# Two layers of graph attention in f32: q, k and v of two batches in one product, weight pieces fetched from DRAM as they are used

## The chip, the cores and the metric

One core of a Trainium2 chip. The time is device microseconds of one execution, the median of three: 2844.64 us for the kernel before (2844.39 to 2846.03). All numbers are f32; nothing is computed in a narrower type.

## What is computed

64 batches of 256 tokens with 512 features pass two layers:

```python
q, k, v = x @ Wq + bq, x @ Wk + bk, x @ Wv + bv          # 8 heads of 64
scores = q k^T / 8 + (1 - adj) * -1e9                     # 256 x 256 a head
x = layernorm(x + softmax(scores) v @ Wo + bo)
h = x @ W;  s1 = h a1;  s2 = h a2
e = leaky_relu(s1[:, None] + s2[None, :], 0.2) * adj
x = layernorm(x + elu(softmax(e) h + beta h))
```

Five products with a 512x512 matrix are taken per batch: q, k, v, o and u. The second layer mixes x by its softmax first, with beta on the diagonal ("spread"), and multiplies by W after ("u"); W a1 and W a2 are folded into two rows once.

## The kernel before

**Seven products for eight.** A 512x512 product is split in halves on three sides (features in, features out, tokens); by a Strassen-Winograd scheme it takes seven products of halves in place of eight. The left sides (weights) are W11, W12, W22 and four sums; weight_sums (line 337) makes the sums once and keeps them in SBUF, and writes W21 + W22 over W21. The right sides are quarters of the transposed tokens xT and three sums of them, made per batch by token_sums (line 351) with four subtractions on GpSimd. project (line 370) runs the seven products into three PSUM tiles (chain, cross, pair), each followed by a copy (ACT) or an add (DVE) into a quarter of the result. For q and k the result lies by feature: the stationary side is a 128x128 block of the weights and 128 tokens stream past it, four matmuls a product (line 383). For v, o and u the tokens are stationary and 256 features stream, two matmuls a product (line 388). Only batch 0's q and k are taken the plain way (plain_qk, line 550).

**A batch's stages.** x (transposes of x, L535), q, k, scores (eight heads, two at a time in two row halves of the array, L637), exp and mask on ACT and DVE, v, sums (denominators by a matmul with ones, L660; reciprocal on DVE; out to DRAM and back on every partition by three DMAs of SP, L675 and L679), mix (weights times v, L614), o, normalization (L482 to L492), logits (L813 on DVE, L823 on PE), softmax, attention (L859), spread, u, finish (L516 to L522).

**The order.** Nothing is issued as it is written. Every step is recorded with Plan.op: its engine, a cost in ns, the buffers it reads, writes and claims. Plan.place (line 107) then puts them in order. PE's order is given: each PE step belongs to a turn (round, place in ROUND), and line 503 says in which round after its own a stage of batch b runs (x two rounds early, q and k one early, u two late), so that one round holds stages of five batches and every result has other stages to hide behind. All other engines are filled by a list scheduler: earliest start first, then the due time that follows from PE's order. Buffers come from pools with a fixed number of slots (line 236: 9 of the size of a 256x512 tile, 24 of half that, 8 PSUM banks); a step waits for a slot. The last 60 PE steps are free of the turns. SP issues all large DMAs in one queue, in the order that place gives.

One round takes 43.77 us, the same to 0.01 us from batch to batch. From the timeline of PE, with the start of each stage: sums 1400.67, mix 1401.67, scores 1405.28, q 1408.93, attention 1415.29, v 1415.72, spread 1421.77, o 1424.92, u 1430.96, k 1437.01, x 1443.26, logits 1444.13, next sums 1444.44.

**Beginning and end.** The first round loads x and the weights, makes the weight sums, res_sb (bo + bv Wo, residual_bias, line 438, four matmuls of 128x512), the mask and the second layer's rows. The last batch takes plain products for o and u and spreads its reciprocals by matmul. If any denominator is out of range, a second pass in another form follows; it does not run here.

The lines that set the old order:

```python
ROUND = ("sums", "mix", "scores", "q", "attention", "v", "spread", "o", "u", "k", "x", "logits")
...
            later = {"x": -2, "q": -1, "k": -1, "scores": 0, "v": 0, "sums": 1, "mix": 1, "o": 1, "logits": 1,
                     "attention": 2, "spread": 2, "u": 2}[what]
            plan.turn = (n + later, ROUND.index(what))
```

Of the kernel before, what the change touches and what calls it, by code (L numbers as in the profile page):

```python
# [11 lines left out]
AF = mybir.ActivationFunctionType  # L12
# [4 lines left out]
P = 128  # L17
# [5 lines left out]
ROUND = ("sums", "mix", "scores", "q", "attention", "v", "spread", "o", "u", "k", "x", "logits")  # L23
# [199 lines left out]
def gnn_two_layers(ctx: ExitStack, tc: tile.TileContext, x, adj, Wq, bq, Wk, bk, Wv, bv, Wo, bo, W, a, beta, out):  # L223
# [12 lines left out]
    slots = {"x": 5, "full": 9, "half": 24, "xS": 4, "st": 90, "ps": 8, "rows": 4}  # L236
# [42 lines left out]

    def weight(w, name):  # L280
        w_sb = once([C, D], name)
        for c in range(C):
            plan.op("SP", 1000, lambda c=c: nc.sync.dma_start(w_sb[:, c], w[blk(c), :]), [], [(w_sb, c)])
        return w_sb
# [18 lines left out]
    wq_sb = weight(Wq, "wq_sb")  # L303
    wk_sb = weight(Wk, "wk_sb")
# [46 lines left out]
    def token_sums(T, keys, name):  # L351

        S = sb("xS", [3, 2, P], name)
        q = {(k, j): (lambda k=k, j=j: T[:, 2 * k:2 * k + 2, blk(j)]) for k in range(2) for j in range(2)}
        t2, t3, t4 = ((lambda i=i: S[:, i]) for i in range(3))

        def sub(dst, p, m, reads, writes):  # L360
            plan.op("POOL", 725, lambda: nc.gpsimd.tensor_tensor(dst(), p(), m(), ALU.subtract), reads, writes)  # L361

        sub(t3, q[1, 1], q[0, 1], [keys(1, 1), keys(0, 1)], [(S, 1)])
        sub(q[0, 1], q[0, 1], q[0, 0], [keys(0, 1), keys(0, 0)], [keys(0, 1)])
        sub(t2, q[1, 1], q[0, 1], [keys(1, 1), keys(0, 1)], [(S, 0)])
        sub(t4, q[1, 0], t2, [keys(1, 0), (S, 0)], [(S, 2)])
        return [(q[0, 0], [keys(0, 0)]), (q[1, 0], [keys(1, 0)]), (q[1, 1], [keys(1, 1)]), (t4, [(S, 2)]),
                (q[0, 1], [keys(0, 1)]), (t2, [(S, 0)]), (t3, [(S, 1)])]

    def project(left, right, by_feature, claims, copy, add, inner=2):  # L370

        shape = [2, P] if by_feature else [F]
        chain, cross, pair = ps(shape, "ps_chain"), ps(shape, "ps_cross"), ps([2] + shape, "ps_pair")

        def product(n, dst, start):
            l, r = left[n - 1][0](), right[n - 1][0]()
            if by_feature:  # L380
                for f in range(2):
                    for c in range(inner):
                        nc.tensor.matmul(dst[:, f, :], l[:, c, blk(f)], r[:, c, :],  # L383
                                         start=start and f == 0 and c == 0, stop=c == inner - 1,
                                         skip_group_check=True)
            else:
                for c in range(2):
                    nc.tensor.matmul(dst, r[:, c, :], l[:, c, :], start=start and c == 0, stop=c == 1,  # L388
                                     skip_group_check=True)

        def pe(n, buf, part, start, after=()):
            acc = (lambda: buf[A]) if part is None else (lambda: buf[:, part])
            key = (buf, part)
            plan.op("PE", 448 * inner if by_feature else 870, lambda: product(n, acc(), start),
                    left[n - 1][1] + right[n - 1][1] + list(after), [key], claims=claims)
            return key, acc

        copy((0, 0), pe(1, chain, None, True))
        copy((1, 1), pe(5, cross, None, True))
        add((0, 0), pe(2, pair, 0, True))  # L400
        copy((0, 1), pe(6, chain, None, False))
        add((0, 1), pe(3, cross, None, False))
        copy((1, 0), pe(4, pair, 1, False, [(pair, 0)]))
        acc = pe(7, chain, None, False)
        add((1, 1), acc)
        add((1, 0), acc)

# [30 lines left out]
    def residual_bias():  # L438
        bo_sb = for_now(bo, 0, "bo")
        acc = ps([D], "ps_b")  # L440

        def pe():
            for c in range(C):
                nc.tensor.matmul(acc[A], bv_sb[:, c:c + 1].to_broadcast([P, P]), wo_sb[:, c, :], start=c == 0,
                                 stop=c == C - 1)

        plan.op("PE", 3440, pe, [wo_sb], [acc], claims=[res_sb])
        plan.op("DVE", 690, lambda: nc.vector.tensor_add(res_sb[A], acc[A], bo_sb[A]), [acc, bo_sb], [res_sb])
        return weight_sums(wo_sb, "so_sb", "POOL", [res_sb])
# [46 lines left out]
    def batch(b, at, general=False):  # L496

        X = sb("x", [NT, D], f"x_{b}")
        n = b or 0

        def turn(what):

            later = {"x": -2, "q": -1, "k": -1, "scores": 0, "v": 0, "sums": 1, "mix": 1, "o": 1, "logits": 1,
                     "attention": 2, "spread": 2, "u": 2}[what]
            plan.turn = (n + later, ROUND.index(what))

        plan.op("SP", 2800, lambda: nc.sync.dma_start(X[A], x[at].rearrange("o (t p) d -> p (o t) d", p=P)), [],
                [(X, (t, i)) for t in range(NT) for i in range(2)], first=b == 0)

# [3 lines left out]
        def finish(t, us, u, mode):  # L513
# [9 lines left out]
                out[at].rearrange("o (t p) d -> p (o t) d", p=P)[:, t, :], X[:, t, :]), tokens(t), [])  # L523


        xT, qT, kT = (sb("full", [C, N], f"{n}_{b}") for n in ("xT", "qT", "kT"))
        last = b == B - 1 and not general
        V = sb("full", [NT, D], f"v_{b}")

        def tr_x(t):  # L530
            tr = ps([C, P], "tr_x")

            def pe():
                for c in range(C):
                    nc.tensor.transpose(tr[:, c, :], X[:, t, c * P:(c + 1) * P], ident)  # L535

            plan.op("PE", 430, pe, tokens(t), [tr], claims=[xT])
            plan.op("ACT", 680, lambda: nc.scalar.copy(xT[:, :, blk(t)], tr[A]), [tr], [(xT, t)])

            plan.op("POOL", 1270, lambda: nc.gpsimd.tensor_tensor(X[:, t, :], X[:, t, :], res_sb[A], ALU.add),  # L540
                    [res_sb], tokens(t))

        if b == 0:
            plan.turn = (0, ROUND.index("spread"))
            left["o"] = residual_bias()
        turn("x")
        for t in range(NT):
            tr_x(t)

        def plain_qk(w, bias, dst):  # L550

            accs = [ps([2, N], "ps_plain") for _ in range(2)]
            for c in range(C):
                def pe(c=c):
                    for f in range(C):
                        nc.tensor.matmul(accs[f // 2][:, f % 2, :], w[:, c, blk(f)], xT[:, c, :],  # L556
                                         start=c == 0 and f % 2 == 0, stop=c == C - 1, skip_group_check=True)

                plan.op("PE", 1740, pe, [xT, (w, c)], accs, claims=[dst])
            for f in range(C):  # L560
                plan.op("ACT", 370, lambda f=f: nc.scalar.activation(
                    dst[:, f, :], accs[f // 2][:, f % 2, :], AF.Identity, bias=bias[:, f:f + 1]),
                    [accs[f // 2]], [(dst, (f // 2, j)) for j in range(NT)])

        if b == 0:
            turn("q")
            plain_qk(wq_sb, bq_sb, qT)
            turn("k")
            plain_qk(wk_sb, bk_sb, kT)
            left["q"] = weight_sums(wq_sb, "sq_sb", "DVE")  # L570
            left["k"] = weight_sums(wk_sb, "sk_sb", "DVE")
            left["v"] = weight_sums(wv_sb, "sv_sb", "POOL")
        right = token_sums(xT, lambda k, j: (xT, j), "xS")

        def gather(quarter, bias=None):

            def copy(q, acc):
                (dst, key), (src, acc) = quarter(q), acc[::-1]
                if bias is None:
                    plan.op("ACT", 400, lambda: nc.scalar.copy(dst(), src()), [acc], [key])  # L580
                    return
                for f in range(2):
                    plan.op("ACT", 350, lambda f=f: nc.scalar.activation(
                        dst()[:, f, :], src()[:, f, :], AF.Identity,
                        bias=bias[:, 2 * q[0] + f:2 * q[0] + f + 1]), [acc], [key])

            def add(q, acc):
                (dst, key), (src, acc) = quarter(q), acc[::-1]
                plan.op("DVE", 420, lambda: nc.vector.tensor_add(dst(), src(), dst()), [acc, key], [key])  # L589

            return copy, add

        def qk(left, bias, dst):
# [404 lines left out]
```

## Time and profile before

| | |
|---|---|
| median of 3 | 2844.64 us |
| the profiled execution | 2844.93 us, its span 2843.2 us |
| granted TensorE clock | 0.998 |
| busy: PE / weight loads / DVE / ACT / POOL | 2819.6 / 2489.7 / 2092.7 / 1403.3 / 1790.3 us |
| DMA | 111.04 MB, mean 39 GB/s |
| first matmul, last start of a matmul group | 5.01 us, 2831.89 us |

PE is the matmul engine and PEld its weight loads, which run beside it. A row of the timeline is a run of like instructions: start, duration to its end, engine, line, operation, tile written <- tiles read, stationary and moving shapes, count. Each f32 matmul leaves two records, so x8 there is four matmuls of the code. Since matmuls overlap, the time of a group on PE is the distance from its start to the next start. A row of waits says which instruction waited for which: total us, how often, the longest. A row of windows gives the stretch, its length, busy time and count for PE, PEld, DVE, ACT and POOL, granted clock, share of the DMA engines, GB/s.

### The profile page before, as it was taken

The numbers are of one execution on the slowest core, as the hardware profiler recorded it, in microseconds if no ns is written. First come the engines' busy times: TensorE is split into PE (matmuls) and PEld (weight loads), VectorE is DVE, ScalarE is ACT, GpSimd is POOL, SyncE is SP. The second block draws the span as 40 slices with busy tenths as digits, with TensorE's granted clock in tenths as the row PEclk, the third lists the DMA queues.
The fourth block names the chain that finished last, engine by engine and source line by source line (L and its number), as shares of the span: only waits on it lengthen the run. The fifth ranks groups of instructions, "written<-read, shape, count | busy, mean of one in ns | idle before, by whom it ended". The sixth has DMA issues, their size and how long they took to land.

```text
span 2843.2 us, 54507 instructions
## 1 busy us (share of the span) xinstructions
PE 2819.6 (99%) x20313; PEld 2489.7 (88%) x20313; DVE 2092.7 (74%) x4498; ACT 1403.3 (49%) x3507; POOL 1790.3 (63%) x2507
## 2 busy tenths in 40 slices
PE   9999999999999999999999999999999999999997
PEld 7888888988888889888888898888888888888885
DVE  5767777777677777776777777767777777677786
ACT  4445445455454554544545545445445454454453
POOL 6666566566665665666656666666566666666654
PEclk9999999999999999999999999999999999999999
DMA  3011011011110110111101101011011010110100
GB/s 134 21 33 46 24 46 46 23 46 36 33 46 24 46 46 24 46 34 35 46 24 45 46 23 46 33 36 46 24 46 46 24 46 32 37 46 24 49 31 27
DMA packets 75645, 111.04 MB, mean 39 GB/s; under 512 B 6136, under 2 KB 39664, under 8 KB 75376
## 3 DMA queue, kind: packets, MB, share of 16 engines
q1 hardware_dynamic: 75248, 107.49, 11.7%
q8 instruction: 163, 2.67, 0.4%
q14 instruction: 106, 0.87, 0.1%
q0 software_dynamic: 128, 0.01, 0.0%
HBM read 73.41 MB, written 34.07 MB: 38 GB/s over the span
## 4 chain that ended last, share of the span: by engine, by line
PE 98%; DVE 1%; POOL 0%; issue 0%; ACT 0%; POOLq 0%; DVEq 0%
PE ps_chain L388 17%; PE ps_chain L383 15%; PE ps_cross L388 12%; PE ps_pair L388 12%; PE ps_pair L383 10%; PE ps_cross L383 10%; PE ps_sc L637 8%; PE ps_pv L614 8%; PE ps_den L660 2%; PE tr_x L535 2%; PE tr_a L859 1%; PE ps_plain L556 1%; PE tr_s L823 1%; DVE junk L813 0%; PE ps_plain L423 0%
## 5 line engine op out<-in xcount | busy, mean ns | idle before, releaser
L648 POOL TENSOR_TENSOR both<-pT 128x256 f32<-128x256 f32 x512 | 362.1, 734 | 151.6 <-ACT pT L646 151.6
L644 DVE TENSOR_TENSOR pT<-ps_sc,maskT_sb 128x512 f32<-128x512 f32 x512 | 316.8, 680 | 11.7 <-PE ps_sc L637 5.5
L580 ACT COPY u<-ps_chain 128x256 f32<-128x256 f32 x126 | 46.9, 372 | 511.3 <-PE ps_chain L388 511.3
L540 POOL TENSOR_TENSOR x<-x,res_sb 128x512 f32<-128x512 f32 x128 | 164.1, 1283 | 201.0 <-PE tr_x L535 199.8
L646 ACT ACTIVATE pT<-pT 128x512 f32<-128x512 f32 x512 | 287.2, 624 | 3.8 <-DVE pT L644 3.8
L813 DVE SCALAR_TENSOR_TENSOR junk<-x,wa_sb 128x512 f32<-128x512 f32 x256 | 261.6, 1074 | 0.0
L486 POOL TENSOR_SCALAR rs<-mv 128x1 f32<-128x1 f32 x256 | 55.4, 217 | 324.5 <-DVE mv L483 319.9
L637 PE MATMUL ps_sc<-qT,kT 64*128 64x256 f32 x2048 | 238.4, 382 | 0.0
L614 PE MATMUL ps_pv<-pT,v 128*64 128x256 f32 x2048 | 235.1, 382 | 0.0
L637 PEld LDWEIGHTS ps_sc<-qT,kT 64*128 64x128 f32 x2048 | 192.8, 187 | 44.3 <-issue 24.0
L614 PEld LDWEIGHTS ps_pv<-pT,v 128*64 128x64 f32 x2048 | 141.4, 137 | 90.7 <-issue 26.1
L492 ACT ACTIVATE x<-x,nmr,rs 128x512 f32<-128x512 f32 x256 | 194.1, 806 | 5.5 <-DVE nmr L490 5.3
L361 POOL TENSOR_TENSOR yS<-yT 128x256 f32<-128x256 f32 x126 | 91.8, 729 | 152.1 <-DVE yT L589 147.1
L482 DVE BATCH_NORM_STATS2 bn<-x 128x6 f32<-128x512 f32 x256 | 170.6, 687 | 4.4
L899 POOL TENSOR_TENSOR X_sums<-x 128x256 f32<-128x256 f32 x126 | 119.4, 948 | 85.0 <-ACT x L492 85.0
L487 POOL TENSOR_TENSOR rs<-rs,neg_half 128x1 f32<-128x1 f32 x256 | 144.3, 564 | 21.3
L700 ACT COPY oT<-ps_pv 128x512 f32<-128x512 f32 x128 | 75.0, 587 | 150.6 <-PE ps_pv L614 150.5
L790 DVE TENSOR_TENSOR x<-x,ps_chain 128x256 f32<-128x256 f32 x252 | 100.3, 418 | 63.8 <-PE ps_chain L388 56.9
L383 PE MATMUL ps_chain<-xS,sk_sb 128*128 128x128 f32 x1008 | 133.1, 275 | 0.0
L383 PE MATMUL ps_chain<-xS,sq_sb 128*128 128x128 f32 x1008 | 133.1, 275 | 0.0
L388 PE MATMUL ps_chain<-sv_sb,xS 128*128 128x256 f32 x512 | 131.4, 379 | 0.0
L388 PE MATMUL ps_chain<-sw_sb,yS 128*128 128x256 f32 x504 | 130.2, 381 | 0.0
(222 smaller groups left out, 7697.3 us busy)
## 6 DMA issues: line engine op xcount, KB each, us to landing
x<-in_x_dram SPq DMA_DIRECT2D x64, 512.0 KB, 4.5
out_dram<-x SPq DMA_DIRECT2D x128, 256.0 KB, 2.0
inv_all<-rows SPq DMA_DIRECT2D x126, 256.0 KB, 3.6
wq_sb<-in_L_gnn_Wq_dram SPq DMA_DIRECT2D x4, 256.0 KB, 5.7
wk_sb<-in_L_gnn_Wk_dram SPq DMA_DIRECT2D x4, 256.0 KB, 7.6
wv_sb<-in_L_gnn_Wv_dram SPq DMA_DIRECT2D x4, 256.0 KB, 7.4
wo_sb<-in_L_gnn_Wo_dram SPq DMA_DIRECT2D x4, 256.0 KB, 5.1
w_sb<-in_L_gnn_W_dram SPq DMA_DIRECT2D x4, 256.0 KB
```

What stands on the lines that cost most here:

```text
L383: nc.tensor.matmul(dst[:, f, :], l[:, c, blk(f)], r[:, c, :], start=start and f == 0 and c == 0, stop=c == inner - 1, skip_group_check=True)
L388: nc.tensor.matmul(dst, r[:, c, :], l[:, c, :], start=start and c == 0, stop=c == 1, skip_group_check=True)
L482: plan.op("DVE", 690, lambda: nc.vector.bn_stats(bn[A], X[:, t, :]), [(X, (t, 0)), (X, (t, 1))], [bn])
L487: nc.gpsimd.tensor_tensor(rs[A], rs[A], neg_half, ALU.pow)
L492: plan.op("ACT", 810, lambda: nc.scalar.activation(X[:, t, :], X[:, t, :], AF.Identity, bias=nm[A], scale=rs[A]), [nm, rs], [(X, (t, 0)), ...
L540: plan.op("POOL", 1270, lambda: nc.gpsimd.tensor_tensor(X[:, t, :], X[:, t, :], res_sb[A], ALU.add), [res_sb], tokens(t))
L614: nc.tensor.matmul(acc[s * HD:(s + 1) * HD, i, :], V[:, k, h * HD:(h + 1) * HD], pT[h][:, k, :], start=k == 0, stop=k == NT - 1)
L637: nc.tensor.matmul(acc[i + s][:, k, :], kT[r:r + HD, h // 2, blk(k)], qT[r:r + HD, h // 2, :], start=True, stop=True)
L644: plan.op("DVE", 690, lambda h=h, i=i: nc.vector.tensor_add(pT[h][A], acc[i][A], maskT_sb[A]), [acc[i], maskT_sb], [pT[h]])
L646: plan.op("ACT", 620, lambda h=h: nc.scalar.activation(pT[h][A], pT[h][A], AF.Exp, scale=1.0 / HD ** 0.5), [pT[h]], [pT[h]])
L648: plan.op("POOL", 725, lambda h=h: nc.gpsimd.tensor_tensor(both[h // 2][:, h % 2, :], pT[h][:, 0, :], pT[h][:, 1, :], ALU.add), [pT[h]], [ ...
L813: plan.op("DVE", 780, lambda t=t, i=i, junk=junk: nc.vector.scalar_tensor_tensor(junk[A], X[:, t, :], 1.0, wa_sb[:, i, :], op0=ALU.mult, o ...
```

## The change

Batches are taken in pairs. x of both is loaded, transposed and put side by side in xT (token half t of both batches together), so that q, k and v of a pair are one project each with 256 tokens to a half: 256 columns stream for q and k, and v has two stationary blocks a product. The four PSUM tiles (second and fourth in place of one pair tile) fill a bank each. Attention and the second layer stay by batch, s = 0 and 1, reading their columns out of the shared tiles. ROUND is rewritten for two batches, and scores become four steps of two heads.

To make room, Wq, Wk and their sums no longer stay in SBUF: the sums go to DRAM once, and each product's left side (256 KB) is fetched into one of six slots when it is due. The x of a batch that the residual needs is loaded a second time, apart from the one that is transposed (two slots of "xin"). The first pair's q and k use the seven products too, in another order (raw). residual_bias sums bv Wo on DVE first and needs one matmul in place of four. Slots: 4 + 6 double-sized + 18 half-sized in place of 9 + 24.

```diff
-ROUND = ("sums", "mix", "scores", "q", "attention", "v", "spread", "o", "u", "k", "x", "logits")
+ROUND = ("sums1", "mix1", "scores0", "v", "o1", "attention0", "u0", "spread0", "x", "logits1",
+         "sums0", "mix0", "scores1", "q", "attention1", "o0", "spread1", "k", "logits0", "u1")
+
+LATER = {"x": -1, "q": -1, "k": -1, "v": 0, "scores0": 0, "scores1": 0, "sums0": 0, "sums1": 1, "mix0": 0, "mix1": 1,
+         "o0": 0, "o1": 1, "logits0": 0, "logits1": 1, "attention0": 1, "attention1": 1, "spread0": 1, "spread1": 1,
+         "u0": 2, "u1": 1}
...
-    slots = {"x": 5, "full": 9, "half": 24, "xS": 4, "st": 90, "ps": 8, "rows": 4}
+    slots = {"xin": 2, "x": 4, "two": 6, "xP": 1, "piece": 6, "full": 4, "half": 18, "xS": 2, "st": 80, "ps": 8, "rows": 4}
...
+    def streamed(w, w_dram, name):
...
+        kept = Buf(dram_pool, name, [4, P, D], name)
...
+        for n in (1, 2, 3, 4):
+            plan.op("SP", 800, lambda n=n: nc.sync.dma_start(kept[n - 1], S[n][A].rearrange("p c f -> p (c f)")),
+                    [S[n]], [(kept, n)])
+        raw = {1: (0, 0), 2: (0, 1), 4: (1, 1)}
+
+        def fetch(n):
+
+            piece = sb("piece", [2, F], f"{name}_{n}")
+            if n in raw:
+                i, c = raw[n]
+                plan.op("SP", 800, lambda: nc.sync.dma_start(
+                    piece[A], w_dram[2 * c * P:2 * (c + 1) * P, half(i)].rearrange("(c p) f -> p c f", p=P)), [],
+                    [piece])
+            else:
+                k = {5: 1, 6: 2, 7: 3, 3: 4}[n]
+                plan.op("SP", 800, lambda: nc.sync.dma_start(piece[A].rearrange("p c f -> p (c f)"), kept[k - 1]),
+                        [(kept, k)], [piece])
+            return (lambda: piece[A]), [piece]
...
         def product(n, dst, start):
-            l, r = left[n - 1][0](), right[n - 1][0]()
...
+            l, r = sides[n][0](), right[n - 1][0]()
+            for f in range(2 if by_feature else width // P):
+                for c in range(inner):
+                    lhs, rhs = (l[:, c, blk(f)], r[:, c, :]) if by_feature else (r[:, c, blk(f)], l[:, c, :])
+                    nc.tensor.matmul(dst[:, f, :], lhs, rhs, start=start and f == 0 and c == 0, stop=c == inner - 1,
                                      skip_group_check=True)
...
+        copy((0, 0), pe(1, chain, True))
+        if raw:
+            add((0, 0), pe(2, second, True))
+            copy((1, 0), pe(4, fourth, True))
+        copy((1, 1), pe(5, cross, True))
...
-        plan.op("PE", 3440, pe, [wo_sb], [acc], claims=[res_sb])
+        plan.op("PE", 870, lambda: nc.tensor.matmul(
+            acc[A], ones[:, 16:17].to_broadcast([P, P]), part[A], start=True, stop=True), [part], [acc], claims=[res_sb])
...
+        for s in range(2):
+            for t in range(NT):
+                plan.op("SP", 1400, lambda s=s, t=t: nc.sync.dma_start(Xs[s][:, t, :], dram(x, s)[:, t, :]), [],
+                        tokens(s, t), first=m == 0 and s == 0 and t == 0)
...
+            project(left, right, True, [dst], *gather(
+                lambda q: (lambda: dst[:, 2 * q[0]:2 * q[0] + 2, q[1] * N:(q[1] + 1) * N], (dst, q)), bias, True),
+                width=N, raw=m == 0)
...
+        def own(T, r, c):
+
+            return T[r:r + HD, c, :].rearrange("p (t s n) -> p t s n", t=NT, s=2)[:, :, s, :]
...
+        plan.op("SP", 2800, lambda: nc.sync.dma_start(X[A], dram(x, s)), [], tokens(0) + tokens(1))
+        for t in range(NT):
+            plan.op("POOL", 1270, lambda t=t: nc.gpsimd.tensor_tensor(X[:, t, :], X[:, t, :], res_sb[A], ALU.add),
                     [res_sb], tokens(t))
```

## The prediction, as it was put on record

> **What bounds the kernel now.** I read the slices of the span first, then the chain that ended last, then PE's timeline in the middle and at both ends, then the waits of the SP queue.
>
> ```profile
> PE   9999999999999999999999999999999999999997
> DMA  3011011011110110111101101011011010110100
> ```
> ```profile
> PE 98%; DVE 1%; POOL 0%; issue 0%; ACT 0%; POOLq 0%; DVEq 0%
> ```
> ```profile
> 100.00:2740.00 2640.00, 2640.00 (x19172) 2341.41 (x19172) 1961.14 (x4218) 1321.93 (x3316) 1680.31 (x2356) 1.00 0.12 37
> ```
>
> In the 40 slices PE falls short only in the last, and the DMA engines are nearly free after the first. The chain that ended last is PE's own work, 98% of it. The last line is a window from 100 to 2740 us: PE is busy in all 2640 us, at granted clock 1.00; DVE 74%, POOL 64%, ACT 50%, the DMA engines 12%. So the time is the sum of PE's spacings, plus what happens at the two ends. No other engine is worth anything until it makes PE wait. The question is therefore what each PE instruction costs, and that is not its "mean ns" (matmuls overlap) but the distance between starts:
>
> ```profile
> 1415.72 1.03 PE L388 MATMUL ps_chain<-wv_sb,xT 128*128 128x256 f32 x4
> ...
> 1421.77 0.61 PE L383 MATMUL ps_chain<-attT,x 128*128 128x128 f32 x4
> ...
> 1437.01 1.05 PE L383 MATMUL ps_chain<-xT,wk_sb 128*128 128x128 f32 x8
> ...
> 1443.26 1.04 PE L535 MATMUL tr_x<-ident,x 128*128 128x128 f32 x8
> ```
>
> The trace shows each f32 matmul as two records, so x8 is four matmuls. The seven k products of one batch (4 matmuls, 128 columns each) take 1443.26 - 1437.01 = 6.25 us, 0.893 each, 223 ns a matmul. The seven v products (2 matmuls, 256 columns) take 1421.77 - 1415.72 = 6.05 us, 0.864 each, 432 ns a matmul. The same arithmetic costs 3% less in 256-column pieces.
>
> **The steady part.** q and k of two batches become one product of 256 columns: four matmuls in place of eight. The exact form (stationary a weight block, 256 columns of xT) is already in the trace, in batch 0's k:
>
> ```profile
> 17.40 7.07 PE L556 MATMUL ps_plain<-xT,wk_sb 128*128 128x256 f32 x32
> 24.31 1.04 PE L535 MATMUL tr_x<-ident,x 128*128 128x128 f32 x8
> ```
>
> 16 matmuls in 6.91 us, 432 ns each, so 1.728 us a product. A pair saves 2 x 0.893 - 1.728 = 0.058 us per product; 14 products make 0.80 us (the unrounded starts), and 31 pairs (1 to 31) **24.8 us**. v keeps its count and form (14 products of 2 matmuls become 7 of 4): nothing. Scores keep their sixteen matmuls in the same sequence, only cut into four operations; their moving side becomes two runs of 128 columns, which I take at nothing: cost bounded by one extra matmul start per scores matmul, 223 x 2 - 432 = 14 ns x 1024 = 14 us at the worst, and no gain, since nothing is left out. Mode switches stay at the same number per batch.
>
> The Trainium skill speaks on this ("TensorE: Matmul & The Clock Gate", Back-to-back issue gap): a warm isolated matmul is spaced N/2.4 + 2.5 ns. Taken four times for f32 it gives 223 ns at 128 columns, as here, but 437 at 256, where the trace has 432; by the page a pair's product would save 40 ns and the steady part, as an estimate, 17 us. The measured spacing decides.
>
> **The first pair.** Before: q of batch 0 from 7.62 to 16.96, k to 24.31, later q and k of batch 1 (6.35 + 6.25, 12.6 with its switch) and their two transposes (0.87). After: all four transposes come first, then q and k of both. The transposes began at 5.01, waiting for a constant of POOL, and until about 12 us PE ran at half its rate (five records per 2 us in the window 10 to 12, ten in the next). Four transposes at 0.87 bring 8.5, a copy to xT makes q start near 8.7; x of both batches and Wq are 2 MB, and the table of windows has 1.7 MB moved by 8 us and 2.1 by 10, so data is not later. One product at half rate ends at 12.1, the second at 13.9; the third needs the last of four POOL subtractions of 128x512 (1.27 each, row L344) from 9.2: 14.4. It and the four behind it (5 x 1.73 = 8.6) end at **23.0; with 0.4 for the mask's transpose and 12.1 for k, 35.5**, against 24.31 before: +11.2, minus 12.6, minus 0.87 = **-2.3 us**. The residual bias goes from eight records of 128x512 (41.33 to 44.76, 3.43) to two (0.86): **-2.6**; its four DVE steps run while PE does k. Round 1 lacks u of an earlier pair, so between o and logits of batch 1 PE has only 0.43 + 3.15 + 1.74 = 5.3 us of work, where the trace's first such stretch needed 7.7 (o's end 79.70 to the second row at 87.42): a stall of 2.3 in place of 0.33, **+2.0**. At the end, the built order of PE puts four more u products behind the last denominators and 3 us of them before the weighted sum; the chain from there grows as the work in front of it shrinks: **+0.3**.
>
> **What must stay hidden.** Each pair now fetches 14 pieces of 256 KB and 1 MB of x a second time: 4.7 MB per 87 us, 54 GB/s on top of 37. At the start the window 12 to 24 us moved 400 GB/s while PE kept 432 ns a matmul, so transfers do not slow PE. Landing times from the list of DMA issues:
>
> ```profile
> x<-in_x_dram SPq DMA_DIRECT2D x64, 512.0 KB, 4.5
> out_dram<-x SPq DMA_DIRECT2D x128, 256.0 KB, 2.0
> inv_all<-rows SPq DMA_DIRECT2D x126, 256.0 KB, 3.6
> SPq L675 <- DVE nmr L490: 2330.4, 60, 42.7
> ```
>
> The last line, from SP's waits, warns: SP is in order and stands up to 42.7 us at the store of the denominators; all pieces now queue behind such waits. A piece's price, 256 KB in, lies between 2.0 (the same size out) and 4.5 (twice the size in); I take 3.6. In the built order SP has per pair: rows, inv_all, two stores, x, four x loads, rows, inv_all, then the seventh q piece, two k pieces, two stores, three k pieces, x, two k pieces, six pieces of the next q. (The eight stored sums of the first pair are read first at q of pair 1, past 60 us.) Six slots let six pieces come a stage early; the seventh waits for product 1 and is needed five products later, 5 x 1.73 = 8.6 us, against 0.4 (issue) + 4.5. From q's end to k there are 0.43 + 6.05 + 3.15 = 9.6 us. Both hold, so **0**; if not, see the second rival.
>
> The skill has a rule against such pieces ("DMA: Bandwidth & Descriptors", Bandwidth: batch DMAs to at least 1 MiB for 75% of peak; fixed part about 2.0 us). As an estimate it gives 2.6 us for 256 KB, and nothing to the sum either way; the start's 256 KB loads moved 400 GB/s.
>
> POOL's four subtractions of xT take 4 x 1.27 = 5.1 us per pair in place of 2 x 4 x about 0.92, in the same 8.7 us between transposes and q; the last of them is needed only at the sixth product, 8.6 us later, so its cover is double. DVE's adds become 16 of at most 0.69 in place of 32 of 0.42. The tightest place I find is v, which now follows scores of batch 0: it needs a PSUM bank, and scores took all eight. In the built order DVE has, from u's end, two adds (0.75), two L517 (1.35), the reciprocal (1.72), two L519 (1.43), statistics (1.59), a small reciprocal (0.17): 7.0, and the first mask add frees a bank at 7.7. PE comes to v at 1408.93 - 1400.67 = 8.3. Slack 0.6 us.
>
> **Sum**, against the profiled execution's 2844.93 (0.3 above the median 2844.64): -24.8 - 2.3 - 2.6 + 2.0 + 0.3 = -27.4, so 2817.5; with 0.3 taken off 2817.2. I say 2817.
>
> **Rivals.**
> 1. Small stalls each round. If DVE comes 0.3 to 1.0 us later than my tally (two-port operations stretch beside POOL: L813 is 0.68 or 1.2 in the same batch), PE waits for the bank at v 0.1 to 0.5 us per pair: +3 to +15, 2820 to 2832. Against it: PE waited nowhere in 2640 us under similar loads. Chance 0.20, counted from 2824 to 2838.
> 2. The other side: the SP queue starves PE. The mechanism is the in-order queue: pieces of k behind a store that waits for ACT's normalization of batch 0 of the pair before. Place: the first product of k, or the seventh of q. Price: one landing per pair, 2.0 us at least: 31 x 2.0 = +62, 2879; at 4.5, 2957. It decides from 27.4 / 31 = 0.88 us per pair. For it: the 42.7 us wait, and one wait of 28.9 us at a store (L522). Against: 9.6 and 8.6 us of cover. 0.10.
> 3. No gain: 128-column matmuls bound by something that doubling does not remove (PEld is 88% busy), or stalls that eat it: 2839 to 2850. Batch 0's k at 432 ns speaks against. 0.06.
>
> **How the numbers follow.** Forecast, 2811 to 2824: 0.61. Better than 2811 (no startup stall and a tail with fewer gaps): 0.03. Rival 1: 0.20. Rival 2: 0.10. Rival 3: 0.06. The range 2811 to 2834 takes the forecast and most of rival 1; the scores' 14 us fit in it. Within 0.2% (5.7 us, about what a measurement of this kernel can tell from no change) lies rival 3: same 0.06; slower 0.10; faster 0.84.
>
> **What would show it.** Right: PE busy without gaps in the middle; products of q and k at 1.73 us start to start, one round of a pair at 86.7 us against 87.5; first scores near 36 us; one gap near logits in the first 140 us. Rival 1: a wait of v's first matmul on DVE, 31 times. Rival 2: PE waits on a DMA of a piece. Wrong altogether: a spacing of 256-column q products above 1.75 us.

## The result, and the profile after

The changed kernel takes **2830.49 us** (median of 4 runs, 2828.47 to 2830.73), the kernel before 2844.85 on the same chip (4 runs, 2844.39 to 2846.03): ratio 0.9947, 95% interval 0.993 to 0.9965. That is 14.4 us less, not 27.4. The forecast's own case reached to 2824; the time falls where rival 1 was put (2824 to 2838), but not by its mechanism. The stated range (2811 to 2834) takes in most of that rival, and that it holds the result is in part luck. The profiled execution is the fastest of the four: 2828.47 us, span 2826.7, so 16.5 less than the profiled one of before.

The slices of the page, PE and DMA engines:

```profile
PE   9999999999999999999999999999999999999997
...
DMA  6223322232222333323322223333233322232211
```

PE looks as before, and the DMA engines are two and a half times as busy (30% for 12% in the windows of the middle) and still far from full. The steady part, from the timeline of PE (start, length, operation, count of records), seven k products and the step behind them:

```profile
2680.75 1.89 PE L433 MATMUL ps_chain<-xT,wk_sums 128*128 128x256 f32 x8
...
2692.84 0.38 PE L893 MATMUL tr_s<-ident,s 128*128 128x128 f32 x2
```

Seven products take 2692.84 - 2680.75 = 12.09 us, 1.727 each. Two starts of the same stage one pair apart, and a long window (length, busy time and count of PE, PEld, DVE, ACT, POOL, clock, DMA share, GB/s):

```profile
1484.73 1.07 PE L737 MATMUL ps_den<-both,ones 128*32 128x256 f32 x16
...
1571.48 1.07 PE L737 MATMUL ps_den<-both,ones 128*32 128x256 f32 x16
```
```profile
300.00:2600.00 2300.00, 2300.00 (x13910) 1957.85 (x13909) 1760.46 (x3403) 1096.42 (x2393) 1450.80 (x1972) 1.00 0.30 92
```

A round takes 86.75 us against 87.54 (2 x 43.77), and PE never stands. The pieces land sooner than I had put them (3.6 us):

```profile
wq_sums<-wq_sums SPq DMA_DIRECT2D x124, 256.0 KB, 2.6
wk_sums<-wk_sums SPq DMA_DIRECT2D x124, 256.0 KB, 2.8
```

So the middle gives what was forecast, and what is missing lies at the ends. The waits of PE over the whole span (waiting line, what it waited for: us, times, longest):

```profile
PE tr_s L893 <- DVE junk L883: 5.1, 5, 1.9
...
PE ps_chain L433 <- DVE pT L721: 1.6, 1, 1.6
```

**Rounds 0 to 2.** PE stands at 63.95 (1.60), 123.28 (.73), 124.35 (.35), 129.91 (.84), 132.10 (1.90) and 162.27 (.74): 6.2 us. Behind the fourth and fifth the granted clock falls (0.57 from 133 to 137 us): the weighted sum takes 5.14 us where it otherwise takes 3.67, the denominators 1.24 for 1.07. Together 7.8 us.

```profile
129.91 0.29 PE L893 MATMUL tr_s<-ident,s 128*128 128x128 f32 x1 [0.84 <-DVE junk L883]
132.10 0.32 PE L893 MATMUL tr_s<-ident,s 128*128 128x128 f32 x1 [1.90 <-DVE junk L883]
...
133.52 5.14 PE L691 MATMUL ps_pv<-pT,v 128*64 128x256 f32 x32
```

**The last round.** The last scores (batch 63) are cut in two, and then o of batch 62 stands:

```profile
2740.54 2.86 PE L714 MATMUL ps_sc<-qT,kT 64*128 64x256 f32 x24
2746.02 1.73 PE L714 MATMUL ps_sc<-qT,kT 64*128 64x256 f32 x8 [2.62 <-DVE pT L721]
2751.14 2.07 PE L433 MATMUL ps_pair<-wo_sb,oT 128*128 128x256 f32 x4 [3.40 <-DVE pT L721]
```

What DVE did meanwhile, from its own timeline:

```profile
2739.89 2.35 DVE L656 SCALAR_TENSOR_TENSOR x<-u,x 128x512 f32<-128x512 f32 x2
2742.17 1.28 DVE L658 SCALAR_TENSOR_TENSOR x<-m,x 128x512 f32<-128x512 f32 x2
...
2745.31 1.25 DVE L721 TENSOR_TENSOR pT<-ps_sc,maskT_sb 128x512 f32<-128x512 f32 x2
...
2747.27 1.30 DVE L782 TENSOR_TENSOR oT<-oT,inv_all 128x512 f32<-128x512 f32 x2 [0.63 <-DMA inv_all<-rows]
...
2750.41 3.07 DVE L721 TENSOR_TENSOR pT<-ps_sc,maskT_sb 128x512 f32<-128x512 f32 x5
```

DVE first closes batch 58 (L656, L658), then does two mask adds, then waits 0.63 us for the reciprocals that come through DRAM, and only behind the steps that follow them does it come to the other adds, which free the PSUM banks of scores.

### The profile page after: what moved, and what is told of

The parts are those of the page before. It is cut to its first block, busy times and chain, and to the rows that moved or that the text cites. A ratio compares the mean times of both kernels' runs of the same rounds, so it can differ in the third digit from the quotient of the medians.

```text
span 2826.7 us, 47456 instructions
## 1 busy us (share of the span) xinstructions
PE 2793.3 (99%) x16771; PEld 2367.1 (84%) x16771; DVE 2136.6 (76%) x4126; ACT 1319.3 (47%) x2875; POOL 1753.7 (62%) x2379
## 4 chain that ended last, share of the span: by engine, by line
PE 97%; DVE 1%; POOL 0%; DMA 0%; ACT 0%; issue 0%; SPq 0%; DVEq 0%; POOLq 0%; ACTq 0%
PE ps_chain L433 32%; PE ps_cross L433 21%; PE ps_pair L433 10%; PE ps_sc L714 8%; PE ps_pv L691 8%; PE ps_fourth L433 6%; PE ps_second L433 6%; PE ps_den L737 2%; PE tr_x L593 2%; PE tr_a L929 1%; DVE junk L883 1%; PE tr_s L893 0%; PE ps_plain L497 0%; DVE junk L538 0%; DMA xin<-in_x_dram 0%
## 5 line engine op out<-in xcount | busy, mean ns | idle before, releaser
L723 ACT ACTIVATE pT<-pT 128x512 f32<-128x512 f32 x512 | 308.0, 630 | 123.2 <-DVE pT L721 122.0
L883 DVE SCALAR_TENSOR_TENSOR junk<-x,wa_sb 128x512 f32<-128x512 f32 x256 | 246.4, 1015 | 0.7 <-ACT x L566 0.7
L714 PEld LDWEIGHTS ps_sc<-qT,kT 64*128 64x128 f32 x2048 | 199.6, 187 | 43.6 <-issue 24.2
L911 POOL TENSOR_TENSOR e<-e,adj_sb 128x512 f32<-128x512 f32 (+1 forms) x65 | 91.5, 1408 | 205.9 <-DVE e L908 205.9
L969 POOL TENSOR_TENSOR att_sums<-attT 128x128 f32<-128x128 f32 x126 | 57.7, 458 | 203.0 <-ACT attT L933 191.7
L933 ACT COPY attT<-tr_a 128x512 f32<-128x512 f32 x64 | 37.5, 586 | 277.7 <-PE tr_a L929 277.6
L564 DVE SCALAR_TENSOR_TENSOR nmr<-mv,rs 128x1 f32<-128x1 f32 x256 | 102.0, 408 | 72.5 <-POOL rs L561 72.1
L469 ACT COPY yT<-ps_chain 128x256 f32<-128x256 f32 x126 | 46.9, 373 | 231.4 <-PE ps_chain L433 225.2
L404 POOL TENSOR_TENSOR xS<-xT 128x512 f32<-128x512 f32 x64 | 87.4, 1366 | 90.3 <-ACT xT L596 87.8
L404 POOL TENSOR_TENSOR oS<-oT 128x256 f32<-128x256 f32 x126 | 92.5, 734 | 64.1 <-DVE oT L782 59.2
```

The source lines that it names most:

```text
L404: plan.op("POOL", 180 + 545 * width // P, lambda: nc.gpsimd.tensor_tensor(dst(), p(), m(), ALU.subtract), reads, writes)
L714: nc.tensor.matmul(acc[j][:, k, :], kT[r:r + HD, c, key_blk(k)], own(qT, r, c), start=True, stop=True)
L723: plan.op("ACT", 620, lambda h=h: nc.scalar.activation(pT[h][A], pT[h][A], AF.Exp, scale=1.0 / HD ** 0.5), [pT[h]], [pT[h]])
L883: plan.op("DVE", 780, lambda t=t, i=i, junk=junk: nc.vector.scalar_tensor_tensor(junk[A], X[:, t, :], 1.0, wa_sb[:, i, :], op0=ALU.mult, o ...
L969: plan.op("POOL", ns, lambda: nc.gpsimd.tensor_tensor(dst(), p(), m(), op), reads, writes)
```

## The experiments

Changes are against the changed kernel, whose 2830.49 us is what each is compared with. The kernel before took 2844.5 to 2844.8 us beside all of them.

**e1_split: is it the width?**

```diff
+                    for h in range(2 if by_feature and width == N else 1):
+                        to, mv = (dst[:, f, blk(h)], rhs[:, blk(h)]) if by_feature and width == N else (dst[:, f, :], rhs)
+                        nc.tensor.matmul(to, lhs, mv, start=start and f == 0 and c == 0 and h == 0,
+                                         stop=c == inner - 1, skip_group_check=True)
```

> The q and k products keep everything of the changed kernel (pair at once, streamed pieces, order), but each matmul of 256 columns is issued as two of 128. Theory (the steady gain is the matmul's width and nothing else): by the spacings in the trace of the kernel before (0.893 us for four matmuls of 128 columns, 1.728 for four of 256) each of the 14 products of a pair becomes 2 x 0.893 = 1.786 us, 0.058 longer; 31 pairs x 14 x 0.058 = 25 us, so 2830.5 + 25 = about 2856 us, with PE without a gap in the middle and a round of a pair at 87.55 us in place of 86.75. Rival (the gain came from fewer, larger steps: fewer mode changes, fewer evictions, fewer copies): 2830 to 2834, a round of a pair near 86.75.

2857.24 us (2855.45 to 2860.28), 26.8 more. Two k products of its timeline:

```profile
1482.95 1.95 PE L435 MATMUL ps_chain<-xT,wk_sums 128*128 128x128 f32 x16
1484.74 1.95 PE L435 MATMUL ps_cross<-xT,wk_sums 128*128 128x128 f32 x16
```

1.79 us a product, a round 87.58 us, as in the kernel before (87.54): the rounds make 25.9 us of the loss (31 x 0.835). The steady gain is the width of the matmul and nothing else.

**e2_tail: the reciprocals' trip through DRAM.** `near = b >= B - 2` in place of `last` for the two steps that spread reciprocals by matmul.

> Batch 62 spreads its reciprocals by a matmul as batch 63 does, so in the last round no DVE step stands behind a DMA of reciprocals. Theory (the last round's loss is DVE's in-order queue: the multiplication L782 waits for a DMA that lands at 2747.2 and stands ahead of five mask adds that free the banks of scores): the two PE gaps of 2.62 and 3.40 us in the scores of batch 63 go, and with them some 2.7 us of matmuls at half rate; the added spread is PE work of under 1 us: 6 to 8.7 us less, 2822 to 2825. Rival (DVE has simply more work in the last round than PE gives it time for): the gaps stay or move, 0 to 2 us less, 2828.5 to 2830.5.

2833.66 us (2831.57 to 2835.06), 3.2 more: a miss for the theory, and above the rival's range too. The scores run without a gap, but PE now waits for the reciprocal and the copy behind it on DVE, at the new matmul ahead of them, and later at nine other places (0.46 to 2.18 us), where the changed kernel has four behind its last scores and o:

```profile
2740.33 3.62 PE L769 MATMUL ps_inv<-inv,select 128*128 128x256 f32 x8 [2.85 <-DVE select L750]
```

**e3_start: round 1.** L538 gets `mode="two"`, and:

```diff
+            if m == 0 and (what, s) in (("logits", 1), ("attention", 0)):
+                plan.turn = (1, ROUND.index({"logits": "scores1", "attention": "v"}[what]) + 0.5)
```

> Two edits in the first two rounds: the sums for the second layer's rows (L538, two inputs from SBUF on DVE) are kept off the times in which POOL runs, and in round 1 the logits of batch 1 and the attention of batch 0 come later in PE's order (after scores of the second batch, after v). Theory (the lost time of round 1 is PE work too short between o and logits, and DVE steps that stretch from 0.68 to 1.75 us beside POOL): of the gaps 1.60, .73, .35, .84, 1.90 and .74 us with their matmuls at half rate, 7.8 us in all, 4 to 6 go: 2824.5 to 2826.5. Rival (the chain from round 1's normalization to logits is as long wherever it stands, so the gap only moves): within 1.5 us of the changed kernel, 2829 to 2832.

**2825.74 us** (2825.62 to 2826.17), 4.8 less; against the kernel before 0.9931 (0.9915 to 0.9948). It is the fastest kernel of this study. From 95 to 185 us these gaps are left:

```profile
138.76 0.43 PE L895 MATMUL tr_s<-ident,s 128*128 128x128 f32 x2 [1.34 <-DVE pT L723]
139.35 1.99 PE L433 MATMUL ps_chain<-xT,wq_sums 128*128 128x256 f32 x8 [0.16 <-DVE pT L723]
...
159.38 0.71 PE L433 MATMUL ps_cross<-attT,X_sums 128*128 128x128 f32 x4 [0.74 <-POOL attT L971]
```

The gain is the order alone. The edit to L538 did nothing: four of these steps still take .90 to 1.75 us, and the gap of 1.6 us at q of pair 1 stays (1.61). e10_both, below, has the order without that edit. From the first denominators to the fourth PE takes 129.5 us in the changed kernel and in e9_u_early, and 124.9 in e3_start and in e10_both: 4.6 less, with the edit and without.

**e4_twice: streaming doubled.** Each fetch of a piece is followed by the same fetch into a spare buffer.

> Every piece of a left side is fetched twice, the second time into a buffer that nobody reads: 14 more DMAs of 256 KB per pair in SP's queue, 3.7 MB more per round. Theory (streaming is hidden: pieces land in 2.6 to 2.8 us and are issued up to six products early): 0, 2829 to 2832, PE without a gap in the middle. Rival (the SP queue is near its limit): PE waits on a DMA of a piece at the seventh q product or at k, at least 0.5 us per pair, 2846 or more.

3120.62 us (3119.47 to 3121.97), and **the experiment failed as a test**. Nothing waits for the copies, so the planner put them, 114 MB, at the beginning:

```profile
DMA  9999932322233323232223333323223333332211
```

For the first 390 us the DMA engines are over 90% busy, and PE waits 126.3 us for a block of Wq. All is lost in the first 411 us, and nothing from there to the last round: the first product of spread in round 1 comes 288.3 us later than in the changed kernel (411.58 for 123.28), and the last round 288.2 later. It says nothing of pieces fetched twice in the middle.

**e8_three: streaming with less cover**, in its place: `"piece": 3` for 6.

> Three slots for streamed pieces in place of six; nothing else. A piece can then be asked for when the product three before it has ended, 2 x 1.73 = 3.46 us before it is needed, against a landing 2.6 to 2.9 us after its issue and a semaphore and an issue of some tenths. Theory (six slots cover a piece's landing several times, and the queue in SP brings nothing on top): 3.46 is just enough, 0 to 0.2 us for each of about 8 products a pair, so 2830 to 2880 us, any wait of PE being at q and k products on a DMA of a piece. Rival (pieces stand behind the waits of stores and of the reciprocals in SP's queue, and only the six slots hide it): a wait of several us each pair, more than 2900 us.

2882.85 us (2881.57 to 2885.59), 52.4 more and 2.9 above what the theory allowed. The waits of PE:

```profile
PE ps_cross L433 <- POOL attT L969: 23.0, 31, 1.1
PE ps_chain L433 <- DMA wq_sums<-wq_sums: 8.2, 25, 0.6
```

The rows count 8.2 us of waits for a piece, always at the last q product; the loss is larger than what they count. A round takes 88.41 us for 86.75, and by the starts of its stages on PE (mean of 28 rounds) it is all in two of them: q takes 12.81 for 12.19, spread 7.29 for 6.25. So pieces cost 0.62 us a round, some 19 us in all. The larger part, 1.04 a round, is the planner's: on POOL the sums of attention now stand behind the adds of x, and spread waits for them in every round. So 3.46 us of lead falls short by some tenths. Six slots add the time of three products, 5.2 us, and should have over 4 to spare, an estimate from these rows; no wait behind the stores in SP's queue shows.

**e6_bias: four matmuls again** for bv Wo (the function of before).

> The residual bias is made by four matmuls of 128x512 again, as in the kernel before; everything else as changed. Theory (these matmuls stand on PE's path at the start, 3.43 us in the trace of the kernel before against 0.86 in that of the changed one): 2.6 us more, 2832 to 2834. Rival (PE waits at the start anyway, in round 1, for DVE and x, so the time comes back): 0, 2829.5 to 2831.

2832.02 us (2829.98 to 2833.30), 1.5 more: at the lower edge of the theory's range, and some of the runs overlap with those of the changed kernel. The matmuls take 3.44 us (52.86 to 56.30) for .86, but the wait of 1.60 us at q of pair 1 is gone. So by the two traces the change saved 2.6 us there, and 1.6 of them came back as a wait for DVE some 10 us later.

**e7_early and e7_earlier: the last scores forward.** In the last round, sums0, mix0, scores1 follow o1, or v:

```diff
+            if m == B // 2 - 1 and f"{what}{s}" in ("sums0", "mix0", "scores1"):
+                plan.turn = (m, ROUND.index("o1") + {"sums": 0.2, "mix": 0.4, "scores": 0.6}[what])
```

> In the last round alone, sums, mix of batch 62 and scores of batch 63 move forward in PE's order, from behind the logits to behind o of batch 61. Theory (the end is set by the chain of the last batch, from the end of its scores to the end of the span: 2764.83 to 2843.2 = 78.4 us in the kernel before, 2747.75 to 2826.7 = 78.9 in the changed one, 79.4 with batch 62's reciprocals spread by matmul, 79.2 with the other start; what lies behind the scores matters little): the scores would end near 2734 and the chain at 2813, but PE's own work then binds: 104.7 us busy from 2700 and 11.9 us behind the last matmul give 2816.6 at the least, so 2817 to 2823 us, 6 to 13 less than the changed kernel. Rival (the tail is the sum of DVE's work, whatever the order): 2828 to 2831, the chain behind the last scores grows to 86 us or more.

> The same three stages of the last round still further forward, to behind v of the last pair. Theory (chain of the last batch, then PE's own work): no better than with the stages behind o of batch 61 if PE's work already binds, 2817 to 2823; if the chain of the last batch were all, 6 us less than that run. Rival (sum of DVE's work): 2828 to 2831.

2838.12 us (2836.47 to 2839.88) and 2837.55 (2836.42 to 2839.10): 7.6 and 7.1 more, above the rival's range too. My theory fell: the chain behind the last scores is not fixed, it grew from 79 to 100.5 us (2735.67 to 2836.2). PE now waits in u of batch 58, which comes right behind the scores, for ACT's copy of its first product:

```profile
2743.38 2.08 PE L433 MATMUL ps_chain<-sw_sb,yS 128*128 128x256 f32 x4 [4.34 <-ACT u L469]
```

**e9_u_early: the closing of batch 58 out of DVE's way**, and **e10_both**, the same with e3's order. Here u of batch 58 moves from behind attention of batch 60 to behind v:

```diff
+            if m == B // 2 - 3 and f"{what}{s}" == "u0":
+                plan.turn = (m + 2, ROUND.index("v") + 0.5)
```

> In the last round alone, u of batch 58 moves forward in PE's order, from behind attention of batch 61's forerunner to right behind v; the seven products are the same and still stand ahead of the last scores, which stay where they are. With it the closing steps of batch 58 on DVE (L656, L658, L556: 2739.9 to 2744.6 in the trace of the changed kernel, just when the mask adds of the last scores become due) come earlier, and the recorded order has seven of the eight adds ahead of the multiplication that waits for the reciprocals. Theory (the two gaps of PE in the last scores, 2.62 and 3.40 us, and some 2.7 us of matmuls at half rate, come from DVE's queue: closing steps and a DMA wait ahead of the adds): the first gap goes and the second shrinks, 3 to 8 us less, 2822 to 2827.5. Rival (the packing of the last 60 free steps decides, and any new order packs differently, as with batch 62's spread and with the earlier scores): 2830 to 2838, with the gaps at other places.

> The later logits and attention of round 1 and the earlier u of batch 58 in the last round, together, without the edit to L538. Theory (the two ends add up; the edit to L538 did nothing, since these steps took 1.74 us with it too): 4.7 less than the changed kernel for the start, and what the early u gives alone, 3 to 8: 2818 to 2823. Rival (the L538 edit was what helped at the start, or the tail doesn't mend): 2825 to 2831.

2840.33 us (2839.32 to 2842.84) and 2836.72 (2836.03 to 2837.36): 9.8 and 6.2 more, above both ranges each time. Of the theory only the first half came: the gap in the scores went, but the one at o of batch 62 grew from 3.40 to 4.33, and gaps opened elsewhere, as the rival had it. PE in the last round of e9:

```profile
2740.93 0.45 PE L895 MATMUL tr_s<-ident,s 128*128 128x128 f32 x1 [3.35 <-DVE junk L885]
2743.09 0.48 PE L895 MATMUL tr_s<-ident,s 128*128 128x128 f32 x1 [1.72 <-DVE junk L885]
...
2749.99 3.73 PE L716 MATMUL ps_sc<-qT,kT 64*128 64x256 f32 x32
...
2758.63 2.04 PE L433 MATMUL ps_pair<-wo_sb,oT 128*128 128x256 f32 x4 [4.33 <-DVE oT L784]
```

All eight adds now come ahead of the multiplication, and the scores run in one piece: what cut them was DVE's queue. But u had been the work that covered batch 61's way from o to its logits. Without it PE waits 3.35 and 1.72 us there, as in round 1, where no u exists yet; and the multiplication, now last, holds o for 4.33.

**e11_open90 and e12_open75: a freer end.** `OPEN = 90`, or 75, for 60, in e3_start.

> The kernel of e3_start with one number changed: the last 90 PE steps in place of 60 are free of the turns, so that the planner may order nearly the whole last round by due times. Theory (the last round has no q, k and x, some 27 us less PE work, so its chains through DVE can't all be covered, whatever the order; a gap filled opens elsewhere): within 6 us of 2825.7, 2822 to 2832. Rival (the loss at the end comes from the fixed order of the turns, and freedom mends it): 2815 to 2821.

> The kernel of e3_start with the last 75 PE steps free of the turns in place of 60: the recorded order of the last scores stays, only stages behind them move a little. Theory (as for 90 steps): within 4 us of 2825.7, 2822 to 2830. Rival (fixed turns): 2815 to 2821.

2839.21 us (2836.99 to 2840.42) and 2827.11 (2825.53 to 2827.52). With 75 it is as expected; with 90 it is 13.5 more than e3_start, outside both ranges: waits of 3.68 and 4.17 us stand among others in the last round. The rival fell: freedom doesn't mend it, and here the planner's order by its own costs is worse than the turns.

## Why the prediction was right in the middle and short at the ends

By its own steps, in the profiled execution (2828.47 - 2844.93 = -16.5):

| step | predicted | measured |
|---|---|---|
| steady part, 31 pairs | -24.8 | -24.4 (31 x (87.533 - 86.747), rounds averaged over 29 pairs) |
| first pair | -2.3, first scores at 35.5 | first scores at 35.48 |
| residual bias | -2.6 | 3.43 to 0.86: -2.6 |
| waits of the first rounds | +2.0 | 7.8 in place of 0.33: +7.5 |
| end | +0.3 | +4.5 (counted below) |

As counted the rows make -17.3. The missing 0.8 us lies ahead of the fourth denominators and is not placed.

- **The spacing of 432 ns was the right row**, and what it is worth is shown: e1_split takes it away and loses 26.8 us. That scores, v and the doubled x cost nothing is borne out by its round, which has all of these: 87.58 us against 87.54.
- **Streaming hidden: right.** Pieces land in 2.6 to 2.8 us, and e8_three shows a shortfall of tenths with half the slots. Rivals 2 and 3 are out. The 2.0 us of fixed cost that the prediction took from the Trainium skill stand there ("DMA: Bandwidth & Descriptors", Anatomy of one DMA — SWDGE (gpsimd) path) for DMAs issued from GpSimd; these are issued from SP, and the estimate of 2.6 us is near what they took.
- **Rival 1 did not occur**, though the time lies in its region: v never waits for a bank. Slack of 0.6 us was enough in the middle. (One reading of the first pair was off without effect: the window from 10 to 12 us has six records of PE, not five.)
- **The term that failed first is "+2.0" for round 1.** I had one gap before logits (2.3) and got two there, .84 and 1.90, with a lower clock behind them, and four others. One is the bias again: "its four DVE steps run while PE does k", but that time is not all gained, since PE then comes to q of pair 1 before DVE is through (e6_bias). e3_start takes back 4.6 by order alone.
- **The term that failed second is "+0.3" for the end.** From the denominators of batch 61 to the end the kernel before takes 2843.2 - 2713.67 = 129.5 us. The changed one no longer has q and k of batch 63 there (12.6) and has u of batch 58 more (6.05), so 123.0 would be even; it takes 127.5, and 4.5 is the loss. In that stretch PE waits 10.1 us in place of 8.2, and 13.6 us in place of 11.3 pass behind the start of its last group of matmuls. I read only what the built order put behind the last denominators. The two longest waits, 6.0 us, stand a step earlier, in part in place of waits that the kernel before has later: scores of batch 63 need DVE just when it closes batch 58 and waits for reciprocals. In the kernel before, DVE's order at the last scores is alike, without harm:

```profile
2764.05 3.65 DVE L644 TENSOR_TENSOR pT<-ps_sc,maskT_sb 128x512 f32<-128x512 f32 x6
...
2767.95 1.82 DVE L705 TENSOR_TENSOR oT<-oT,inv_all 128x512 f32<-128x512 f32 x2
2769.70 1.27 DVE L644 TENSOR_TENSOR pT<-ps_sc,maskT_sb 128x512 f32<-128x512 f32 x2
```

  There v stands behind scores on PE and covers it; in the new round q stands there, and the last round has none. Its q, k and x would be 14 x 1.727 + 1.74 = 25.9 us of PE work, where the last round of before lacks 6.36 + 6.25 + 0.87 = 13.5. That this lack is the reason is argued from these rows; shown is that three edits (e2, e7, e9) closed the gap in the scores and each opened others that cost more: from batch 61's denominators to the end PE took 127.5 us in the changed kernel, 131.1 in e2_tail, 135.4 in e7_early, 138.2 in e9_u_early (of the 3.6 in e2_tail, up to 2.9 can be the clock, see below; its runs are 3.2 slower). Whether another order does better stays open.

The other 2 us of the shortfall are that the profiled run was about 2 us faster than the other three. Kernels with the same order at the end differ in this way, too. The 20 us from the last scores on, in the changed kernel and in e8_three (clock third from the end):

```profile
2740.54:2760.54 20.00, 13.98 (x75) 11.22 (x74) 17.07 (x36) 8.43 (x17) 11.61 (x19) 0.83 0.28 79
```
```profile
2793.22:2813.22 20.00, 15.07 (x68) 11.54 (x67) 16.16 (x34) 8.06 (x16) 10.84 (x17) 0.74 0.25 79
```

At clock 0.83 the last round takes 127.4 to 127.7 us (four kernels), at 0.74 it takes 129.9 to 130.4 (e1, e4, e8). That the three other runs of the changed kernel had the slower end is likely (their mean clock is 0.996 for 0.997), but they left no trace. The start differs as well: the first denominators come at 54.03 us in this trace, and at 54.5 to 55.9 in those of e2, e7 and e9, which are changed in the last round alone. How the 2 us divide between the two ends is not shown.

## What to carry to other kernels

Price a steady change by the start-to-start spacing of the very form it brings, if the trace has it anywhere; here that was right to 2%. Then walk the first and the last rounds of the new order stage by stage, asking of every wait hidden in the middle which stage covers it, and whether that stage exists there: a round made twice as large may leave twice the hole. Work that an engine off the path takes over to relieve the bound engine may return as a wait a few us later, and a gap closed by moving cover can open where the cover came from, as in e9_u_early.

## What the runs showed of the hardware

**The clock falls after gaps shorter than I had thought to matter, and not always alike.** From 129.0 to 133.0 us PE was busy 1.26 of 4.0 us, at granted clock 1.00; in the 4 us after that the clock was 0.57, then 1.00 again. The Trainium skill ("TensorE: Matmul & The Clock Gate", What's actually happening) gives half rate after an idle window of about 3.4 us, counted by a free-running window, so that it varies by run. That agrees with 0.83 and 0.74 for one and the same order; but the longest single gap in the first case was 1.90 us, so no gap as long as that window was needed here. Up to 132.35 the only work of PE there, and in the 1.9 us before, is transposes, and no run shows whether these count as busy. A second place, in the last round, has matmuls of scores on both sides of the gap, and the longest gap ahead of the fall is 2.62 us (2743.40 to 2746.02). Clock third from the end:

```profile
2743.00:2747.00 4.00, 1.38 (x10) 0.66 (x7) 3.63 (x9) 1.73 (x6) 1.42 (x4) 1.00 0.56 131
2747.00:2753.00 6.00, 2.60 (x10) 1.82 (x7) 5.73 (x11) 2.95 (x6) 4.24 (x7) 0.56 0.13 51
```

In narrower windows it is 0.95 from 2747.50 to 2747.75, where the scores end, and 0.50 from there on: it falls before the next gap has begun. In e8_three the same gap of 2.62 us (to 2798.70) stands there, and the clock is 0.51 from 2799 on: it falls 0.3 us after the gap in place of 1.7.

**A DVE step with two inputs from SBUF waits for POOL.** Two rows of the changed kernel, the same step (L538) before and while POOL is busy (4.94 of the 5.02 us from 58.20):

```profile
53.94 0.69 DVE L538 SCALAR_TENSOR_TENSOR junk<-w_sb,a 128x512 f32<-128x512 f32 x1
...
59.88 1.74 DVE L538 SCALAR_TENSOR_TENSOR junk<-w_sb,a 128x512 f32<-128x512 f32 x1
```

This is 2.5 times as long. Three steps take 1.74 to 1.75 us and one .90, and the last ends at 63.22, just ahead of the adds that PE waits for at 63.95. The skill has the cause ("SBUF — State Buffer", Who interferes with whom): such an instruction and one of GpSimd that reads SBUF exclude each other on a shared port. The planner knows the rule for steps marked "two"; marking L538 left the four steps beside POOL all the same (e3_start); why is not shown.
